# Where the causal mask of attention's score maxima is added: by TensorE's bfloat16 products, or by VectorE as it takes the maxima

## The chip, the core and the metric

The kernel runs on one core of a Trainium2 chip, in one launch. The metric is device time in microseconds from the launch's first to its last instruction; several runs are made and the median is given. The core's engines run side by side, each with its own queue in program order: TensorE (PE: matmuls, with its weight loads shown as PEld), VectorE (DVE), ScalarE (ACT), GpSimd (POOL) and SyncE (SP, which here issues the DMAs). Matmuls write to PSUM, eight banks of 512 float32 per partition; the other data lie in SBUF.

## What is computed

The reference passes a batch of 8 sequences of 512 tokens by 256 features through six residual layers: a feed-forward layer with four-bit quantisation, a retention layer, that feed-forward layer again, a soft mixture of experts, a causal attention with 16 heads of width 16, and the mixture of experts again. Every layer is preceded by a layer norm. The change touches the attention alone:

```python
scores = jnp.einsum('bhqd,bhkd->bhqk', q, k) / jnp.sqrt(jnp.float32(HEAD_DIM))
causal = jnp.tril(jnp.ones((S, S), dtype=bool))
scores = jnp.where(causal, scores, -jnp.inf)
attn = jax.nn.softmax(scores, axis=-1)
ctx = jnp.einsum('bhqk,bhkd->bhqd', attn, v)
```

with S = 512. Queries and keys come from projections with a low-rank part, which the kernel folds into one weight each.

## The kernel before

**Three lanes.** The program is one long sequence of instructions, written out by a planner while the kernel is built. Three lanes deliver steps: `front` (lane f: feed-forward, retention, feed-forward, and the routing of the first mixture), `back` (lane b: attention and the routing of the second mixture) and `experts` (lane e: the expert products). Lane f works on one sequence while lane b works on another. `Meter` (from line 82) keeps an estimate of when each engine is free and when each piece of data is ready; `drive` (line 1495) takes, among the lanes whose next step could begin, the one that the next letter of the string `ORDER` (line 67) names, and where no letter fits the one that has spent least (`chosen`, line 1464). Small work on VectorE that nobody needs at once is put off and slipped in where the planner sees room (`put_off`, `fill`). Because every instruction goes through the meter, the profile puts almost all of them on line 182; groups are told apart by the names of their tiles.

**PSUM.** It is divided into three pairs of banks (`pair`, line 327, kind "p") and two single banks (`one`, line 330, kind "o"), shared by all lanes. A step says which it needs ("pp" is two pairs) and starts when they are free.

**Attention** (line 1145) goes through a sequence's 16 heads in 4 head groups of 4 heads (index n). The four heads of a group lie in four blocks of 32 partitions, so that four products with a contraction of 32 rows run in TensorE at the same time. Each head group goes through this:

1. `largest(n, k)` for k = 0, 1, 2 (line 1218): the scores s_a, with queries as rows, for the query tiles named by `by_query` (line 1185): tiles 0 and 2 in stage 0, tile 3 in stage 1, tile 1 in stage 2. A query tile i has (i + 1) x 128 keys. `four` (line 1189) takes two pairs, writes each of the four heads into a bank of its own, and then adds the causal mask to the diagonal 128 x 128 block: one more product per head, the identity in bfloat16 (`identb`) against the mask in bfloat16 (`causalb`), accumulated into the same bank. In stage 0 it covers the diagonal blocks of both tiles, 256 columns. Then VectorE reduces: one instruction takes the negated maxima of two heads at once, so there are 4, 2 and 2 reductions in the three stages.
2. `lower(n)` (line 1238): when all three stages are done, VectorE transposes the 32 columns of maxima (`nmx`), four DMAs take them to HBM, and one brings them back as a row of the queries (`qv_a<-mx_a`). The queries hold a row that was left free for it, and the keys a row of ones, so that the next product subtracts the maxima.
3. `weights` and `exponentials` (lines 1258 and 1266) for three stages: the scores again, st_a, now with keys as rows; VectorE adds the float32 mask `causalT` in place (`masked`, line 1213), and ScalarE takes the exponential into pT_a.
4. `values` (line 1275): products with the values into c_a, whose extra column gives the sums; then a transpose on VectorE and the division.

The score stages of head group n + 1 are written between the stages of group n's weights, one each (line 1336), so the maxima are on their way while the previous group is worked on.

The constants are made at the start (lines 378 to 391): the identity, its bfloat16 copy, the two masks.

Of the kernel before, what the change touches and what calls it, by code (L numbers as in the profile page):

```python
# [21 lines left out]
BF = mybir.dt.bfloat16  # L22
I32 = mybir.dt.int32
AF = mybir.ActivationFunctionType
ALU = mybir.AluOpType
AX = mybir.AxisListType
PSUM = bass.MemoryType.PSUM

P = 128
D = 256  # L30
KD = D // P
S = 512
NT = S // P
# [31 lines left out]
SHARE = {"front": 1.0, "back": 0.9, "experts": 1.15}  # L65

ORDER = (
    "fffeeeeeffffbfbfbffbbbfbfffbbbeeeeeeebbfbfbebbfefefefbbebbebbbbfbfbfbfbbebffffbfffbfffffebebfbbfbfbf"
    "bfbebbbbbbbffffbffbfffbbfbbbbffffbfbbfbffbfffffbfbffbfbbfbbbbffffbffbbbfbfffbfbfbbfbfbfbfbfbbfbffbfe"
    "ebbbffbbbbffffffffffffffffffbfbffffbbbfebfeebbfbfffbfbfbbbffffbfbfbffbffbbbffbffbffbfbbffbbbbfffffff"  # L70
    "fffffffffffbbbbbffffffbfbfbbbfffbfffbbfbfbfbfffbbfbffbfbffbfebbbffbfbfbebffffbbbfbfffffffffffffffffb"
    "ffbffbbebebfbfbbbbbffffffbfbbffffffffbfbfebfbbffbffbfbbffbbbbffffffffffffffffffbfbbfbbffffbfbbfbbeff"
    "ffbebffebfbfbffbfffffbfbfbfbbfbfbfbfbfbbbbbbffffbfbffbfbfefffffffffeebebbbfffbbbbfbfbfbfbfffbfbbebbb"
    "fbfbfbbbbbbbbbb"
)

BEHIND = 60.0
# [217 lines left out]
def macaron(ctx: ExitStack, tc: tile.TileContext, a: dict, out: bass.AP):  # L295
    nc = Meter(tc.nc)
    B = out.shape[0]

    const = ctx.enter_context(tc.tile_pool(name="const", bufs=1))
# [27 lines left out]
    def pair(name):  # L327
        return take("p", name, [P, 2, 512])

    def one(name, keep=False):  # L330

        return take("o", name, [P, 512], keep)
# [45 lines left out]
    ident = const.tile([P, P], FP, tag="ident", name="ident")  # L378
    make_identity(tc.nc, ident)

    identb = const.tile([P, P], BF, tag="identb", name="identb")
    nc.vector.tensor_copy(identb, ident)

    causalb = const.tile([P, 2, P], BF, tag="causalb", name="causalb")
    causalT = const.tile([P, P], FP, tag="causalT", name="causalT")
    for t, pattern, cm in ((causalb, [[0, 2], [-1, P]], 1), (causalT, [[1, P]], -1)):
        nc.gpsimd.memset(t, 0.0)
        nc.gpsimd.affine_select(
            out=t, in_=t, pattern=pattern, compare_op=ALU.is_ge, fill=-1e30, base=0, channel_multiplier=cm
        )  # L390
    neghalf = const.tile([P, NS], FP, tag="neghalf", name="neghalf")
    nc.gpsimd.memset(neghalf, -0.5)
# [749 lines left out]
    NG = HPT // 2  # L1142
    VW = HD + 1

    def attention(lane, b, after):
        nm = f"a_{b}"
# [6 lines left out]
        qv, kv, nmx = {}, {}, {}  # L1153
# [15 lines left out]
        ps = pair(f"v_{nm}")  # L1169
# [11 lines left out]
        def rows_of(r):  # L1181
            return slice(32 * r, 32 * (r + 1))
# [3 lines left out]
        by_key = (((0, 0),), ((1, 0), (3, S - P)), ((2, 0),))  # L1186
        NK = len(by_key)

        def four(name, lhs, rhs, parts, mask, between=lambda: None):

            ps = [pair(f"{name}_{g}") for g in range(2)]
            bank = [ps[r // 2][:, r % 2, :] for r in range(NG)]
            for k, (ls, rs, to, _) in enumerate(parts):
                for r in range(NG):
                    nc.tensor.matmul(
                        bank[r][:, to], lhs[rows_of(r), ls], rhs[rows_of(r), rs], start=(k == 0), stop=mask is None and k == len(parts) - 1
                    )
            between()  # L1200
            if mask is None:
                return ps
            first, n = parts[0][3], len(parts)
            for r in range(NG):
                if n == 1:
                    at, m = bank[r][:, first : first + P], mask[:, 0, :]
                else:
                    step = (parts[1][3] - first) // P
                    at, m = bank[r].rearrange("p (c k) -> p c k", k=P)[:, first // P :: step, :], mask
                nc.tensor.matmul(at, identb, m, start=False, stop=True)  # L1210
            return ps

        def masked(ps, starts, by):
# [4 lines left out]
        def largest(n, k):  # L1218

            parts = []  # L1220
            if k == 0:
                nmx[n] = small.tile([P, BLK], FP, tag="nmx", name=f"nmx_{nm}_{n}")
                nc.gpsimd.memset(nmx[n], 0.0)
            for i, c in by_query[k]:
                w = (i + 1) * P
                parts.append((slice(i * P, w), slice(0, w), slice(c, c + w), c + w - P))
            ps = four(f"s_{nm}_{n}_{k}", qv[n], kv[n], parts, causalb)
            for g in range(2):
                for i, c in by_query[k]:
                    nc.vector.tensor_reduce(  # L1230
                        nmx[n][:, : NG * NT].rearrange("p (r i) -> p r i", i=NT)[:, 2 * g : 2 * g + 2, i],
                        ps[g][:, :, c : c + (i + 1) * P],
                        AX.X,
                        ALU.max,
                        negate=True,
                    )

        def lower(n):
# [19 lines left out]
        def weights(n, k, between=lambda: None):  # L1258

            parts, end = [], 0  # L1260
            for j, c in by_key[k]:
                end = c + S - j * P
                parts.append((slice(j * P, (j + 1) * P), slice(j * P, S), slice(c, end), c))
            return four(f"st_{nm}_{n}_{k}", kv[n], qv[n], parts, None, between), end

        def exponentials(n, k, ps, end):
            pT = []
# [7 lines left out]
        def values(n, k, pc, pT):  # L1275

            o, u = divmod(n, 2)
            for j, c in by_key[k]:
                for r in range(NG):
                    at = (j * HEADS + o * HPT + 2 * r + u) * VW  # L1280
                    nc.tensor.matmul(
                        pc[rows_of(r), j * P :],
                        va[:, at : at + 32],
                        pT[r // 2][:, r % 2, c : c + S - j * P],
                        start=(j == 0),
                        stop=(k == NK - 1),
                    )
# [28 lines left out]
        for k in range(NK):  # L1316
            yield "pp", (("qk", nm, 0),), ("s", nm, 0, k)
            largest(0, k)
        lower(0)

        yield "pp", (("qk", nm, 0),), ("s", nm, 1, 0)
        largest(1, 0)
        for n in range(N):
            for k in range(NK):
                if k == 0:
                    yield "ppo", (("q", nm, n), ("v", nm)), ("st", nm, n, k)
                    ps, end = weights(n, k)
                    pc = one(f"c_{nm}_{n}", keep=True)
                else:
                    yield "pp", (("q", nm, n), ("st", nm, n, k - 1)), ("st", nm, n, k)  # L1330
                    ps, end = weights(n, k, lambda: values(n, k - 1, pc, pT))
                pT = exponentials(n, k, ps, end)
                m, l = n + 1 + (k + 1) // NK, (k + 1) % NK
                if m < N and (n or l):
                    yield "pp", (("qk", nm, m // 2),), ("s", nm, m, l)
                    largest(m, l)
                    if l == NK - 1:
                        lower(m)
            yield "", (("st", nm, n, NK - 1), ("v", nm)), ("ctx", nm, n)
            values(n, NK - 1, pc, pT)  # L1340
            z = narrow(lane, f"z_{nm}_{n}", S)
            nc.vector.transpose(z, pc)
            divide_later(n, z)
            drop(f"c_{nm}_{n}")
            if n == 0:
                yield "p", (("yT", nm),), ("qk", nm, 1)
                qk(1)
                yield "pp", (("qk", nm, 1),), ("s", nm, 2, 0)
                largest(2, 0)
        for g in range(NT // 2):  # L1350
            yield "o", tuple(("cx", nm, o) for o in range(KD)), None
            ps = one(f"o_{nm}_{g}")
            for t in (2 * g, 2 * g + 1):
                for d in range(KD):
# [4 lines left out]
                        start=(d == 0),  # L1359
                        stop=(d == KD - 1),  # L1360
# [284 lines left out]
```

## Time and profile before

| What | Value |
|---|---|
| median of 3 runs | 2861.74 us (2860.11 to 2862.71) |
| profiled execution, first to last instruction | 2860.3 us |
| mean granted TensorE clock | 0.992 |
| score products s_a, 1024 instructions | busy 37.2 us (512 wide), 29.1 (384), 24.3 (256), 18.1 (128) |
| transposed score products st_a, 1024 | busy 37.6, 30.7, 26.3, 13.6 us for the same widths |
| loads of the bfloat16 identity, 384 | busy 24.6 us, mean 98 ns |
| TensorE idle until a reduction nmx_a let go | 4.5 us, 7 times |
| VectorE mask additions on st_a, 128x256, 256 | busy 101.3 us, mean 428 ns |
| VectorE idle until s_a was ready | 112.5 us, 57 times |
| ScalarE idle until st_a was masked | 150.0 us, 30 times |

In the page's groups a line has the source line, the engine, the operation, what it writes and reads (with tile names; the suffix tells the layer: _a attention, _m routing, _e experts, _f feed-forward, _r retention), the shapes and the number of instructions; after the first bar the busy time of the group and the mean length of one in ns; after the second the engine's idle time just before them and what ended it. A matmul's length holds its passage through a pipeline, so that lengths of neighbours overlap; what a group costs the queue is seen from the starts. For float32 operands each product is two instructions. The timeline gives the start, the length from the first start to the last end of a merged group, the engine and the operation. The bfloat16 products are one instruction each.

### The profile page before, as it was taken

Reading aid. Unit: us, or ns where it says so; the run is one execution under the profiler, and the core shown is the slowest. Engines: PE = TensorE matmul, PEld = TensorE weight load, DVE = VectorE, ACT = ScalarE, POOL = GpSimd, SP = SyncE. Lnnn points to the kernel's source line nnn. Section 1 sums busy time; section 2 is a strip of 40 time slices with the busy share of each in tenths; the row PEclk is TensorE's granted clock in tenths of the full one; section 3 lists DMA queues with packets and bytes.
Section 4 is the critical chain, followed back from the end, with each engine's and each line's share of the span. In section 5 each row is a group of like instructions: output and inputs, shape, how many; then the busy total and the mean of one; then the engine's idle time right before and its main releaser. Section 6 shows DMA issues by size and latency. Waiting matters only on the chain.

```text
span 2860.3 us, 34542 instructions
## 1 busy us (share of the span) xinstructions
PE 2753.0 (96%) x13166; PEld 1904.5 (67%) x13166; DVE 1675.2 (59%) x3989; ACT 1149.2 (40%) x1549; POOL 126.7 (4%) x260
## 2 busy tenths in 40 slices
PE   4889999999999999999999999999999999999999
PEld 2666677656776677666866667666677666665668
DVE  7787657555565674656746566466756655355440
ACT  2433434434434353433624435244443443434331
POOL 0000000000000000000000000000000000000000
PEclk9999999999999999999999999999999999999999
DMA  4000102110200320002200022000210020102020
GB/s 129 1 1 18 53 1 71 43 37 1 70 1 1 86 71 1 1 1 86 70 1 1 2 85 71 1 1 23 78 56 1 1 71 21 59 1 68 12 78 8
DMA packets 79015, 98.91 MB, mean 35 GB/s; under 512 B 17024, under 2 KB 63872, under 8 KB 78848
## 3 DMA queue, kind: packets, MB, share of 16 engines
q1 hardware_dynamic: 78848, 96.69, 11.5%
q8 instruction: 104, 1.70, 0.3%
q14 instruction: 63, 0.52, 0.1%
HBM read 58.40 MB, written 38.24 MB: 34 GB/s over the span
## 4 chain that ended last, share of the span: by engine, by line
PE 92%; DVE 4%; ACT 3%; issue 1%; DMA 0%; POOL 0%; ACTq 0%; POOLq 0%
PE p_e L182 15%; PE h_e L182 15%; PE gu_f L182 11%; PE lt_m L182 8%; PE mo_e L182 8%; PE sl_m L182 8%; PE dn_f L182 5%; PE s_a L182 4%; PE st_a L182 3%; PE c_a L182 3%; PE qk_a L182 2%; PE y_r L182 1%; PE a_r L182 1%; PE hTp_f L182 1%; PE k_r L182 1%; PE o_a L182 1%
## 5 line engine op out<-in xcount | busy, mean ns | idle before, releaser
L182 PE MATMUL h_e<-slT_m,w1g 128*128 128x256 f32 x2048 | 467.5, 383 | 9.6 <-ACT hid_e L182 4.6
L182 PE MATMUL p_e<-w,hid_e 128*128 128x256 f32 x2048 | 455.1, 381 | 1.5 <-DVE x L182 0.8
L182 PEld LDWEIGHTS h_e<-slT_m,w1g 128*128 128x128 f32 x2048 | 384.9, 191 | 85.1 <-issue 11.1
L182 PEld LDWEIGHTS p_e<-w,hid_e 128*128 128x128 f32 x2048 | 386.0, 190 | 62.1 <-issue 7.3
L182 ACT ACT_TABLE_LOAD x276 | 354.1, 1283 | 180.2 <-PE h_e L182 113.3
L182 PE MATMUL gu_f<-w_in,y_ffn 128*128 128x352 f32 x1024 | 327.0, 472 | 9.2 <-ACT y_ffn L182 8.0
L182 PEld LDWEIGHTS gu_f<-w_in,y_ffn 128*128 128x128 f32 x1024 | 196.7, 195 | 119.6 <-issue 12.9
L182 DVE TENSOR_REDUCE nmx_a<-s_a 128x2 f32<-128x256 f32 (+3 forms) x256 | 196.0, 819 | 113.0 <-PE s_a L182 112.5
L182 ACT ACTIVATE pT_a<-st_a 128x1024 f32<-128x1024 f32 (+1 forms) x192 | 158.8, 877 | 219.9 <-DVE st_a L182 150.0
L182 PE MATMUL lt_m<-yT_m,seT 128*128 128x512 f32 x512 | 231.0, 602 | 7.1 <-DVE lg_m L182 3.3
L182 PE MATMUL mo_e<-proc_e,lg_m 128*128 128x257 f32 x1024 | 234.3, 383 | 1.2 <-DVE x L182 1.2
L182 PE MATMUL sl_m<-ed_m,y_dis 128*128 128x512 f32 x512 | 227.5, 595 | 0.5 <-ACT y_ffn L182 0.5
L182 PEld LDWEIGHTS mo_e<-proc_e,lg_m 128*128 128x128 f32 x1024 | 190.8, 190 | 42.9 <-issue 4.8
L182 ACT ACTIVATE hid_e<-h_e 128x1024 f32<-128x1024 f32 x128 | 131.0, 1024 | 201.4 <-PE h_e L182 200.3
L182 ACT COPY proc_e<-p_e 128x512 f32<-128x512 f32 x64 | 37.5, 586 | 376.2 <-PE p_e L182 376.2
L182 PE MATMUL dn_f<-w_dn,hT_f 128*128 128x256 f32 x768 | 179.7, 386 | 1.1 <-ACT hT_f L182 1.0
L182 PEld LDWEIGHTS lt_m<-yT_m,seT 128*128 128x128 f32 x512 | 96.2, 192 | 121.3 <-issue 102.4
L182 PEld LDWEIGHTS sl_m<-ed_m,y_dis 128*128 128x128 f32 x512 | 96.1, 190 | 111.5 <-issue 102.6
L182 DVE TENSOR_TENSOR h_f<-h_f,gu_f 128x352 f32<-128x352 f32 x128 | 66.4, 519 | 167.1 <-ACT h_f L182 166.5
L182 PEld LDWEIGHTS dn_f<-w_dn,hT_f 128*128 128x128 f32 x768 | 144.5, 194 | 23.1 <-ACT hT_f L182 1.2
L182 DVE TENSOR_SCALAR_CACHE_REDUCE lg_m<-lt_m 128x512 f32<-128x512 f32 x128 | 85.3, 683 | 124.9 <-PE lt_m L182 124.9
L182 DVE TENSOR_TENSOR st_a<-st_a,causalT 128x256 f32<-128x256 f32 x256 | 101.3, 428 | 70.1 <-PE st_a L182 67.0
(190 smaller groups left out, 3132.0 us busy)
## 6 DMA issues: line engine op xcount, KB each, us to landing
d_ed_m<-ed_m SPq DMA_DIRECT2D x256, 128.0 KB
ed_m<-d_ed_m SPq DMA_DIRECT2D x64, 512.0 KB
rb_m<-row_rb_m SPq DMA_DIRECT2D x32, 256.0 KB
x<-in_L_attn_x SPq DMA_DIRECT2D x8, 512.0 KB
tm_m<-row_nm_m SPq DMA_DIRECT2D x16, 256.0 KB
out<-x SPq DMA_DIRECT2D x8, 512.0 KB
row_rb_m<-z_rb_m SPq DMA_DIRECT2D x128, 0.5 KB
mx_a<-z_mx_a SPq DMA_DIRECT2D x128, 2.0 KB
```

Source lines behind the costliest of these rows:

```text
L182: call(*args, **kwargs)
```

## The change

The mask products go. `four` no longer has a mask, and the bfloat16 identity is not made. `causalb` becomes one tile of 128 x 512 in bfloat16: zero in the first 384 columns, the causal pattern in the last 128. In `largest`, the reduction of two heads is replaced by one fused VectorE instruction per head and query tile (`tensor_tensor_reduce`): it adds the last w columns of `causalb` to the head's w columns of scores, multiplies by -1, writes that back in place, and takes the minimum, starting from 3e38, into the head's column of `nmx`. That is the same negated maximum in the same place. So for one head group there are 8, 4 and 4 fused instructions in the three stages. `ORDER` is another string (621 letters instead of 615). The meter's prices are not changed.

```diff
--- before.py
+++ after.py
@@ -65,13 +65,13 @@
 SHARE = {"front": 1.0, "back": 0.9, "experts": 1.15}
 
 ORDER = (
-    "fffeeeeeffffbfbfbffbbbfbfffbbbeeeeeeebbfbfbebbfefefefbbebbebbbbfbfbfbfbbebffffbfffbfffffebebfbbfbfbf"
-    "bfbebbbbbbbffffbffbfffbbfbbbbffffbfbbfbffbfffffbfbffbfbbfbbbbffffbffbbbfbfffbfbfbbfbfbfbfbfbbfbffbfe"
-    "ebbbffbbbbffffffffffffffffffbfbffffbbbfebfeebbfbfffbfbfbbbffffbfbfbffbffbbbffbffbffbfbbffbbbbfffffff"
-    "fffffffffffbbbbbffffffbfbfbbbfffbfffbbfbfbfbfffbbfbffbfbffbfebbbffbfbfbebffffbbbfbfffffffffffffffffb"
-    "ffbffbbebebfbfbbbbbffffffbfbbffffffffbfbfebfbbffbffbfbbffbbbbffffffffffffffffffbfbbfbbffffbfbbfbbeff"
-    "ffbebffebfbfbffbfffffbfbfbfbbfbfbfbfbfbbbbbbffffbfbffbfbfefffffffffeebebbbfffbbbbfbfbfbfbfffbfbbebbb"
-    "fbfbfbbbbbbbbbb"
+    "fffbeeeeffffbfbfbffbbbfbfffbbbbbebbeeebfbefbebbfbfefefbbffebbfbbbfbfbbbbbbbefffffbfffbfffffebebfbbfb"
+    "fbfbfbebbfbbbfffffbffbfbefbfbfffbfbfbbbfbfffbfffffbfbffbfbbfbbbbffbffffbbbebfffbffbbbfbfbfbfbbbfbffb"
+    "feebbbbbbbbbbfbbffffffffffffffbffbfffbbbbbbeebbfbfffffbbbbbffffbfbffffbbfbbbffbfbffbbfbbfbbffffbffef"
+    "ffbbfbbbbfbbbbfbbbbfffffffffbbbffffffbbbfbbbbfffbbffffbfbffbfebbfbfbfffbebffffbbbbbffffbffffffffffff"
+    "bffbffbbfbebebbfbbbbfffbffbfbbffffffffffbbbfeefffbbbfbbfbbfbbbbbbbbbbffbfffbffffbffefbbfbbfffffbfefe"
+    "bfbfbfebfbfebbbbffbffffffbbffffbfbbbfbffbfbfbbbbffffbbfbbffbfeffffbffefbfffffffbfffbffbbfffbbbbbbbbb"
+    "bbfbfbbbbbbfbbbbbbbbb"
 )
 
 BEHIND = 60.0
@@ -378,15 +378,13 @@
     ident = const.tile([P, P], FP, tag="ident", name="ident")
     make_identity(tc.nc, ident)
 
-    identb = const.tile([P, P], BF, tag="identb", name="identb")
-    nc.vector.tensor_copy(identb, ident)
-
-    causalb = const.tile([P, 2, P], BF, tag="causalb", name="causalb")
+    causalb = const.tile([P, S], BF, tag="causalb", name="causalb")
     causalT = const.tile([P, P], FP, tag="causalT", name="causalT")
-    for t, pattern, cm in ((causalb, [[0, 2], [-1, P]], 1), (causalT, [[1, P]], -1)):
-        nc.gpsimd.memset(t, 0.0)
+    nc.gpsimd.memset(causalb, 0.0)
+    nc.gpsimd.memset(causalT, 0.0)
+    for t, step, cm in ((causalb[:, S - P :], -1, 1), (causalT, 1, -1)):
         nc.gpsimd.affine_select(
-            out=t, in_=t, pattern=pattern, compare_op=ALU.is_ge, fill=-1e30, base=0, channel_multiplier=cm
+            out=t, in_=t, pattern=[[step, P]], compare_op=ALU.is_ge, fill=-1e30, base=0, channel_multiplier=cm
         )
     neghalf = const.tile([P, NS], FP, tag="neghalf", name="neghalf")
     nc.gpsimd.memset(neghalf, -0.5)
@@ -1186,28 +1184,16 @@
         by_key = (((0, 0),), ((1, 0), (3, S - P)), ((2, 0),))
         NK = len(by_key)
 
-        def four(name, lhs, rhs, parts, mask, between=lambda: None):
-
-
+        def four(name, lhs, rhs, parts, between=lambda: None):
 
             ps = [pair(f"{name}_{g}") for g in range(2)]
             bank = [ps[r // 2][:, r % 2, :] for r in range(NG)]
-            for k, (ls, rs, to, _) in enumerate(parts):
+            for k, (ls, rs, to) in enumerate(parts):
                 for r in range(NG):
                     nc.tensor.matmul(
-                        bank[r][:, to], lhs[rows_of(r), ls], rhs[rows_of(r), rs], start=(k == 0), stop=mask is None and k == len(parts) - 1
+                        bank[r][:, to], lhs[rows_of(r), ls], rhs[rows_of(r), rs], start=(k == 0), stop=k == len(parts) - 1
                     )
             between()
-            if mask is None:
-                return ps
-            first, n = parts[0][3], len(parts)
-            for r in range(NG):
-                if n == 1:
-                    at, m = bank[r][:, first : first + P], mask[:, 0, :]
-                else:
-                    step = (parts[1][3] - first) // P
-                    at, m = bank[r].rearrange("p (c k) -> p c k", k=P)[:, first // P :: step, :], mask
-                nc.tensor.matmul(at, identb, m, start=False, stop=True)
             return ps
 
         def masked(ps, starts, by):
@@ -1223,16 +1209,15 @@
                 nc.gpsimd.memset(nmx[n], 0.0)
             for i, c in by_query[k]:
                 w = (i + 1) * P
-                parts.append((slice(i * P, w), slice(0, w), slice(c, c + w), c + w - P))
-            ps = four(f"s_{nm}_{n}_{k}", qv[n], kv[n], parts, causalb)
-            for g in range(2):
+                parts.append((slice(i * P, w), slice(0, w), slice(c, c + w)))
+            ps = four(f"s_{nm}_{n}_{k}", qv[n], kv[n], parts)
+            for r in range(NG):
                 for i, c in by_query[k]:
-                    nc.vector.tensor_reduce(
-                        nmx[n][:, : NG * NT].rearrange("p (r i) -> p r i", i=NT)[:, 2 * g : 2 * g + 2, i],
-                        ps[g][:, :, c : c + (i + 1) * P],
-                        AX.X,
-                        ALU.max,
-                        negate=True,
+                    w = (i + 1) * P
+                    own = ps[r // 2][:, r % 2, c : c + w]
+                    at = r * NT + i
+                    nc.vector.tensor_tensor_reduce(
+                        own, own, causalb[:, S - w :], -1.0, 3e38, ALU.add, ALU.min, nmx[n][:, at : at + 1]
                     )
 
         def lower(n):
@@ -1260,8 +1245,8 @@
             parts, end = [], 0
             for j, c in by_key[k]:
                 end = c + S - j * P
-                parts.append((slice(j * P, (j + 1) * P), slice(j * P, S), slice(c, end), c))
-            return four(f"st_{nm}_{n}_{k}", kv[n], qv[n], parts, None, between), end
+                parts.append((slice(j * P, (j + 1) * P), slice(j * P, S), slice(c, end)))
+            return four(f"st_{nm}_{n}_{k}", kv[n], qv[n], parts, between), end
 
         def exponentials(n, k, ps, end):
             pT = []
```

## The prediction

> **What bounds the kernel now.** I read the page first: which engine is full, and whether its clock is. Then the chain that ended last.
>
> ```profile
> span 2860.3 us, 34542 instructions
> PE 2753.0 (96%) x13166; PEld 1904.5 (67%) x13166; DVE 1675.2 (59%) x3989; ACT 1149.2 (40%) x1549; POOL 126.7 (4%) x260
> PE 92%; DVE 4%; ACT 3%; issue 1%; DMA 0%; POOL 0%; ACTq 0%; POOLq 0%
> ```
>
> TensorE is the bound. Its 107 us of idle time lie mostly in the weight preparation: adding up the idle time ahead of TensorE's groups in the timeline from 440 us to the end gives 36.6 us in 2420, so it is 98.5% busy where attention runs (first score at 514 us, last reduction at 2673). A microsecond of matmul removed there is worth a microsecond, as long as nothing new makes TensorE wait. The part of the chain that ended last which covers attention is a sequence of matmul groups too, with single VectorE pieces between.
>
> Next the groups by shape, for the operations that the change takes out, and for those nearest to what it puts in.
>
> ```profile
> L182 PE MATMUL s_a<-causalb,identb 128*128 128x128 bf16 x256 | 25.4, 222 | 0.0
> L182 PE MATMUL s_a<-causalb,identb 128*128 128x256 bf16 x128 | 20.4, 284 | 0.0
> ...
> L182 DVE TENSOR_REDUCE nmx_a<-s_a 128x2 f32<-128x1024 f32 x64 | 75.4, 1220 | 51.4 <-PE s_a L182 51.4
> L182 DVE TENSOR_REDUCE nmx_a<-s_a 128x2 f32<-128x768 f32 x64 | 60.8, 949 | 0.0
> L182 DVE TENSOR_REDUCE nmx_a<-s_a 128x2 f32<-128x512 f32 x64 | 41.2, 686 | 27.8 <-PE s_a L182 27.6
> L182 DVE TENSOR_REDUCE nmx_a<-s_a 128x2 f32<-128x256 f32 x64 | 26.9, 420 | 33.8 <-PE s_a L182 33.6
> L182 DVE TENSOR_TENSOR aT_r<-a_r,dec 128x512 f32<-128x512 f32 x8 | 5.5, 692 | 49.3 <-PE a_r L182 49.3
> L182 DVE TENSOR_TENSOR aT_r<-a_r,dec 128x384 f32<-128x384 f32 x8 | 4.4, 549 | 0.0
> L182 DVE TENSOR_TENSOR aT_r<-a_r,dec 128x256 f32<-128x256 f32 x8 | 3.4, 422 | 3.3 <-PE a_r L182 3.1
> L182 DVE TENSOR_TENSOR aT_r<-a_r,dec 128x128 f32<-128x128 f32 x8 | 2.2, 280 | 0.0
> L182 DVE DVE_READ_ACCUMULATOR lg_m<-lt_m 128x1 f32 x128 | 10.6, 83 | 0.0
> ```
>
> The mask products are 45.8 us of busy time, the reductions 204.3 us. A busy matmul is pipelined, so 45.8 is not what their removal frees. That is read from starts, in the timeline of TensorE around one group (start, length, engine):
>
> ```profile
> 545.03 1.14 PE L182 MATMUL s_a<-kv_a,qv_a 32*128 32x512 f32 x8
> 546.10 0.40 PE L182 MATMUL s_a<-causalb,identb 128*128 128x128 bf16 x4
> 546.34 1.95 PE L182 MATMUL p_e<-w,hid_e 128*128 128x256 f32 x8
> ...
> 623.72 1.14 PE L182 MATMUL st_a<-qv_a,kv_a 32*128 32x512 f32 x8
> 624.79 1.57 PE L182 MATMUL mo_e<-proc_e,lg_m 128*128 128x257 f32 x6
> ```
>
> Scores start at 545.03, the mask 1.07 us later, the next work 0.24 after that. The transposed scores below have the same shape and no mask, and the next full-array matmul starts 1.07 us after them too.
>
> **Term 1, mask products out.** There are 96 groups (8 sequences, 4 head groups, 3 stages). Going through all of them in that timeline, an undisturbed mask holds TensorE for 0.45 us in the 32 groups of stage 0 (four products 256 wide) and 0.235 us in the 64 others (128 wide). 32 x 0.45 + 64 x 0.235 = 29.4 us. The 384 loads of the bf16 identity lie inside these intervals. In 17 groups (2 and 15) TensorE then waits for something anyway, 11.5 us in all, so the mask is covered there: 2 x 0.45 + 15 x 0.235 = 4.4 us that are not won. Net 25 us. The upper end is 34.3 us, the sum of all intervals with their slow cases (0.498 and 0.283 us on average).
>
> The Trainium skill, TensorEngine Tiling (Array Packing), Key Properties, says that a change of tiling mode drains TensorE; by it one could credit a drain saved in each group besides. The two starts of 1.07 us say no: the drain stays with whatever full-array matmul follows. Only where 32-row or 32-column work follows does a switch go (0.54 instead of 0.45 us before c_a), under 1 us in all, which I leave out.
>
> **Term 2, VectorE's work.** Per head group, 8 reductions over two heads each become 16 fused operations over one: in stage 0 four of 128 and four of 384 columns, in stage 1 four of 512, in stage 2 four of 256. With 32 head groups (8 sequences of 4) that is 128 of each width, 512 instead of 256, each with an accumulator to be read out. The trace has no such operation. Three prices:
> - Lowest: like the reduction with accumulator of the dispatch logits (512 wide, from PSUM, followed by an accumulator read). In VectorE's timeline the read comes 0.61 us after the start and the next reduction follows at once. The aT_r rows give (692 - 280) / 384 = 1.073 ns per element, so 0.549 us of stream and 0.06 fixed. Stage 0: 2048 x 1.073 ns + 8 x 0.06 = 2.68 us against 2.49 measured for its four reductions; stage 1: 2.44 against 2.35; stage 2: 1.34 against 1.28. Together 0.34 us more, x 32 = 11 us.
> - Middle: like the mask addition on st_a, in place in PSUM with a second operand: two of 256 in 0.76 us at 536.60, so the second starts 0.76 - 0.428 = 0.33 us after the first, 0.06 fixed; and the accumulator read at its full 83 ns. Stages 3.34, 2.77, 1.67 us: 0.85 + 0.42 + 0.39 = 1.66 more, x 32 = 53 us.
> - Highest: row sums without overlap: 128 x (280 + 422 + 549 + 692) ns + 512 x 83 ns = 291 us against 204.3: 87 us.
>
> I take 53 us, by the row nearest in operands and place. VectorE goes from 59% to about 61%; in the stretch 500 to 650 us it is busy 83.7 of 150 us, and in none of the attention stretches that I looked at over two thirds. It does not become the bound.
>
> What can reach TensorE is the release of PSUM. A score group holds two of the three pairs until its last reduction. Without the mask VectorE can begin 0.45 or 0.24 us earlier, and then takes 0.85, 0.42, 0.39 us longer: the hold grows by 0.40, 0.18 and 0.15 us. Queued behind on VectorE are the mask additions on st_a (ScalarE's exponential waits for them), the logits' reductions and the gate products; and the transpose of the maxima, whose five DMAs on SP's queue bring the row that the next st_a needs, which is fetched a head group ahead. TensorE waits after 17 of 96 groups now: 17 x 0.24 (mean of the three) = 4 us. Its other waits for VectorE from 440 us on sum to 27 us; VectorE's free share falls from 41 to 39%, so about 5% of them, 1.5 us. Both ends: nothing, if the row's price is the lowest; and 17 x 0.6 + 27 us = 37 us if the price is the highest (87 - 29 us of hold over 96 groups = 0.6) and its other waits double.
>
> The Trainium skill, VectorE: DVE Perf Modes, Rules for kernel authors, advises to cut the number of VectorE operations, since each pays a pipeline flush; this change doubles it. With that page's (N + 151) / 0.96 ns for a tensor_tensor the fused operations would be an estimated 251 us before the reads, close to the highest price; the sum would then be some 7 us worse than mine. The 0.33 us from start to start against 428 ns of length shows that part of that flush is overlapped here.
>
> **Small parts, at nothing.** The bf16 identity's cast (304 ns, VectorE) goes; causalb doubles to 512 columns (a 311 ns memset on GpSimd becomes an estimated 0.6). Both lie before 3 us, and TensorE's first matmul starts at 14.0, after the first weights' DMA. Uncovered it would be 0.3 us. The maxima land in the same columns, so the transpose and its DMAs stay as they are.
>
> **The order of the lanes.** It moves whole steps among the three lanes; no instruction count changes. What a row can bound is the idle time that an order leaves: at best part of the 36.6 us, at worst as much again. I take 0: nothing in the profile says which way.
>
> **Sum.** -25 + 4 + 1.5 = -19.5 us on the profiled execution's 2860.3, so 2840.8; the median of the runs is 1.4 us above that span, so **2842 us**. Its own range is 2828 to 2855.
>
> **Rivals.**
> - *More than the sum* (chance 0.15): the mask's whole 34 us and a third of the idle time through the order: 2862 - 34 - 12, about 2815. For it: 79 of the 96 masks are followed by work that waits for nothing. Against: the 17 waits would have to go as well.
> - *No change* (0.10): the saved matmul time turns up as waits for PSUM pairs at once, as in the 17 groups: 2856 to 2867. For it: three pairs only, and score groups take two. Against: the same 79 groups.
> - *VectorE's longer hold decides* (0.27, slower): one place, the last fused operation of a score group before its pair comes free. At the highest price the hold grows by 0.6 us per group; if TensorE meets it in three of four groups, 72 x 0.6 = 43 us against 25 won: 2880. It decides from about 42 groups on (42 x 0.6 = 25), or, at an operation half as fast per element as the rows (32 x 5120 elements x 1.073 ns = 176 us more, 1.8 us per group), from 14 groups on. For it: ScalarE already idles 150 us for the additions on st_a. Against: VectorE itself idles 112.5 us waiting for s_a, which it now gets earlier.
>
> **How the numbers follow.** The forecast has 0.48. Its 0.48 and the first rival's 0.15 are faster; a measurement here tells 0.2%, 5.7 us, from no change, so faster 0.63, same 0.10, slower 0.27. The range reaches down to the first rival's 2815 and up to 2884 in the third; some 0.15 lies outside, mostly above.
>
> **What would show it.** No causalb product on TensorE, and 12 matmuls fewer per head group there; starts of s_a to the next full-array matmul of 1.07 us; 512 fused VectorE operations with a sum of 250 to 295 us with their reads; VectorE at 60 to 62%; TensorE's busy time near 2707 and its idle time within 10 us of 107. I am wrong if the fused row of 512 is well over 0.8 us, if TensorE's waits for nmx_a or for st_a grow past 20 us, or if its idle time moves by more than that in stretches without attention, which would be the order.

## The result, and the profile after

The changed kernel takes 2869.47 us (median of 9 runs, 2868.32 to 2869.97) where the kernel before takes 2861.74 (9 runs, 2860.10 to 2862.74). The ratio is 1.0027, with a 95% interval from 1.0018 to 1.0037: slower by 7.7 us, where 2842 and a gain of 19.5 us were forecast. That is above the forecast's own range (2828 to 2855) and above that of *no change* (to 2867); it lies inside the whole range of 2815 to 2884, in the part that belonged to the third rival.

The page's first lines and its chain, of the changed kernel (busy time, share of the span, instructions):

```profile
span 2867.7 us, 34547 instructions
PE 2735.4 (95%) x12782; PEld 1883.9 (66%) x12782; DVE 1748.1 (61%) x4756; ACT 1130.7 (39%) x1535; POOL 126.3 (4%) x260
PE 86%; DVE 8%; ACT 4%; issue 2%; SPq 0%; DMA 0%; POOL 0%; ACTq 0%; DVEq 0%; POOLq 0%
```

The 384 products are gone, and yet TensorE's busy time falls by 17.6 us (by 31.8 in e1 below, which puts nothing in their place), its idle time grows from 107 to 132 us, and VectorE's part of the chain that ended last doubles from 4% to 8%.

The groups by shape that took the place of the reductions:

```profile
L182 DVE CUSTOM_DVE_ANT_0 s_a<-s_a,causalb 128x512 f32<-128x512 f32 x128 | 87.9, 706 | 47.2 <-PE s_a L182 38.4 <-ACT yT_m L182 3.7 <-ACT pT_a L182 1.3
L182 DVE CUSTOM_DVE_ANT_0 s_a<-s_a,causalb 128x384 f32<-128x384 f32 x128 | 72.5, 566 | 4.4
L182 DVE CUSTOM_DVE_ANT_0 s_a<-s_a,causalb 128x256 f32<-128x256 f32 x128 | 53.7, 439 | 35.0 <-PE s_a L182 32.7
L182 DVE CUSTOM_DVE_ANT_0 s_a<-s_a,causalb 128x128 f32<-128x128 f32 x128 | 39.3, 307 | 48.8 <-PE s_a L182 46.6
L182 DVE DVE_READ_ACCUMULATOR2_ANT nmx_a<- 128x1 f32 x512 | 72.4, 141 | 0.0
```

Each is 14 to 27 ns longer than the aT_r row of its width, and the read that follows takes 141 ns, not 83. How they stand in VectorE's queue is seen from the starts, in its timeline for one stage 1 of the changed kernel:

```profile
522.69 0.70 DVE L182 CUSTOM_DVE_ANT_0 s_a<-s_a,causalb 128x512 f32<-128x512 f32 x1 [3.67 <-ACT yT_m L182]
523.31 0.14 DVE L182 DVE_READ_ACCUMULATOR2_ANT nmx_a<- 128x1 f32 x1
523.49 0.70 DVE L182 CUSTOM_DVE_ANT_0 s_a<-s_a,causalb 128x512 f32<-128x512 f32 x1
524.10 0.14 DVE L182 DVE_READ_ACCUMULATOR2_ANT nmx_a<- 128x1 f32 x1
524.10 0.73 DVE L182 CUSTOM_DVE_ANT_0 s_a<-s_a,causalb 128x512 f32<-128x512 f32 x1
524.75 0.14 DVE L182 DVE_READ_ACCUMULATOR2_ANT nmx_a<- 128x1 f32 x1
524.93 0.70 DVE L182 CUSTOM_DVE_ANT_0 s_a<-s_a,causalb 128x512 f32<-128x512 f32 x1
```

The second operation starts only when the first one's read is over (523.31 + 0.14, then 523.49), the third, which is the first of the second pair of banks, together with the read before it, and the fourth waits again: 0.80, 0.61 and 0.83 us from start to start. Counted from its first start to that of the next instruction, where one follows at once, a stage takes 3.88, 2.85 and 1.96 us (stages 0, 1 and 2, medians) where the reductions took 2.40, 2.27 and 1.32. That is 2.70 us more per head group and 86 us in all.

TensorE's waits for VectorE, in the list of its waits (who waits, for whom, total, times, longest), again of the changed kernel:

```profile
PE h_e L182 <- DVE nmx_a L182: 7.2, 7, 1.3
PE st_a L182 <- DVE nmx_a L182: 7.0, 6, 1.7
...
PE gu_f L182 <- DVE nmx_a L182: 2.4, 2, 1.3
```

That is 16.6 us in 15 waits for a pair that the fused operations still hold, against 4.5 us in 7 waits before.

### The profile page after: what moved, and what is told of

Same layout as the page of the kernel before. It is cut to its first block, busy times and chain, and to the rows that moved or that the text cites. A ratio compares the mean times of both kernels' runs of the same rounds, so it can differ in the third digit from the quotient of the medians.

```text
span 2867.7 us, 34547 instructions
## 1 busy us (share of the span) xinstructions
PE 2735.4 (95%) x12782; PEld 1883.9 (66%) x12782; DVE 1748.1 (61%) x4756; ACT 1130.7 (39%) x1535; POOL 126.3 (4%) x260
## 4 chain that ended last, share of the span: by engine, by line
PE 86%; DVE 8%; ACT 4%; issue 2%; SPq 0%; DMA 0%; POOL 0%; ACTq 0%; DVEq 0%; POOLq 0%
PE p_e L182 15%; PE h_e L182 14%; PE gu_f L182 10%; PE lt_m L182 8%; PE mo_e L182 8%; PE sl_m L182 7%; PE dn_f L182 5%; PE st_a L182 3%; PE c_a L182 2%; PE s_a L182 2%; PE qk_a L182 2%; DVE s_a L182 2%; PE hTp_f L182 1%; PE a_r L182 1%; PE y_r L182 1%
## 5 line engine op out<-in xcount | busy, mean ns | idle before, releaser
L182 PE MATMUL h_e<-slT_m,w1g 128*128 128x256 f32 x2048 | 467.0, 382 | 10.2 <-DVE nmx_a L182 7.2
L182 DVE CUSTOM_DVE_ANT_0 s_a<-s_a,causalb 128x128 f32<-128x128 f32 (+3 forms) x512 | 250.7, 505 | 135.4 <-PE s_a L182 117.8
L182 ACT COPY proc_e<-p_e 128x512 f32<-128x512 f32 x64 | 37.5, 586 | 332.4 <-PE p_e L182 332.4
L182 PEld LDWEIGHTS dn_f<-w_dn,hT_f 128*128 128x128 f32 x768 | 144.1, 193 | 25.3 <-issue 3.1
```

The source lines that it names most:

```text
L182: call(*args, **kwargs)
```

## The experiments

Two things changed together, the work and the order of the lanes. To separate them, the experiments keep the order: a helper tells the planner of the instruction that stood in the old program, and puts another one, or none, in its place. So in each experiment every other instruction of every engine comes in the order of the kernel named.

```python
    def instead(self, name, op, call, *args, **kwargs):
        if name == "PE" and self.kept:
            self.flush()
            self.kept = []
        if name != "PE" and self.kept is not None:
            self.kept.append((name, op, call, args, kwargs))
        else:
            self.emit(name, op, call, args, kwargs)
```

**e1, the products out, nothing in their place.**

```diff
-                nc.tensor.matmul(at, identb, m, start=False, stop=True)
+                nc.instead("PE", "matmul", lambda *x, **y: None, at, identb, m, start=False, stop=True)
...
-        "head_mask": np.where(own, HD**-0.5, 0.0),
+        "head_mask": np.where(own, HD**-0.5 / 4, 0.0),
```

> The kernel before, its instructions in the order of before, without the 384 mask products; the reductions stay. The causal mask of the maxima is left out, and the scores are scaled down by four more so that the sums stay above zero. Theory A (the products hold TensorE for 29 us, and the loss lies in the fused work on VectorE): 2826 to 2840, with TensorE's idle time near 100 us. Theory C (the products were mostly covered, so their removal frees little): above 2852.

Measured: 2841.59 us (5 runs, 2840.48 to 2842.10), ratio 0.9933 (0.9919 to 0.9946), so 18.8 us less than the 2860.41 of the runs beside it. By the starts in TensorE's timeline the work in its queue falls by 31.5 us; its idle time grows by 11 us (102 to 113, both added up from that timeline). So theory C falls, and theory A's price for the masks was somewhat high (its range ended at 2840): a good third of the freed time comes back at once, as waits that the masks had covered.

**e2, the fused operations alone.** The masks stay on TensorE; `zero` is a tile of zeros made at the start.

```diff
-                    nc.vector.tensor_reduce(
+                    def both(*x, g=g, i=i, c=c, nmx=nmx[n], ps=ps, **y):
+                        w = (i + 1) * P
+                        for r in (2 * g, 2 * g + 1):
+                            own = ps[g][:, r % 2, c : c + w]
+                            at = r * NT + i
+                            tc.nc.vector.tensor_tensor_reduce(
+                                own, own, zero[:, :1].to_broadcast([P, w]), -1.0, 3e38, ALU.add, ALU.min, nmx[:, at : at + 1]
+                            )
+
+                    nc.instead(
+                        "DVE", "tensor_reduce", both,
```

> The kernel before with its mask products and in its order; only the 256 reductions become 512 fused operations (they add zeros, as the mask is there already). Theory A (their longer time on VectorE reaches TensorE): 2890 to 2905, TensorE idle 30 to 45 us longer. Theory B (the fused work costs little, the new order of the lanes costs what was won): 2862 to 2870.

Measured: 2884.61 us (4 runs), ratio 1.0084 (1.0070 to 1.0098): 24.2 us more. Less than theory A said, far more than theory B. By the pages TensorE's idle time grows by 14 us (107 to 121), not by 30 to 45; the other 10 us are busy time.

**e3, the change without its order.** The edits of e1 (without the smaller scale) and e2 together, with the causal tile instead of the zeros.

> Masks out of TensorE and into the fused operations, as in the change, but every instruction in the order of before. Theory A: 2862 to 2876, as the changed kernel. Theory B: 2836 to 2848, as I forecast for the change without its order.

Measured: 2874.32 us (5 runs), ratio 1.0046 (1.0034 to 1.0059). Theory A holds.

**e4, the order without the change.** The changed kernel's plan, with the old products and reductions put in place of the fused operations.

> The old work (mask products and reductions of two heads) laid out in the order of the changed kernel. Theory A: 2856 to 2868, the order matters little. Theory B: 2880 to 2895, the order alone costs 20 us or more.

Measured: 2874.61 us (5 runs), ratio 1.0046 (1.0034 to 1.0059). Both expectations missed: the new order costs the old work 14.2 us. The four corners, in us:

| | mask by products | mask by fused operations |
|---|---|---|
| order of before | 2860.4 (kernel before) | 2874.3 (e3) |
| new order | 2874.6 (e4) | 2869.5 (changed kernel) |

The new order is worth 4.9 us to the changed work (6.2 when each is compared with the kernel before of its own session, 2860.4 for e3 and 2861.7 for the changed kernel) and costs 14.2 to the old, so the order is not where the gain went. In the order of before, with the mask off TensorE, going from the reductions (e1) to the fused operations (e3) costs 32.7 us.

**e5 and e6, what in the fused operations costs it.** They add idle work on VectorE to e1, of the length by which the fused operations exceed the reductions: in e5 after a stage's last reduction, where it holds no PSUM, in e6 split before the last reduction of each pair. BEFORE stands for False in e5 and for True in e6; the lines that e5 and e6 share with e1 are left out here.

```diff
+                    def reduced(*x, g=g, i=i, c=c, k=k, **y):
+                        last = i == by_query[k][-1][0]
+                        w = (1330, 605, 560)[k] // (2 if BEFORE else 1)
+                        if BEFORE and last:
+                            tc.nc.vector.tensor_reduce(waste, w_in[:, 0, :w], AX.X, ALU.max)
+                        tc.nc.vector.tensor_reduce(*x, **y)
+                        if not BEFORE and last and g:
+                            tc.nc.vector.tensor_reduce(waste, w_in[:, 0, :w], AX.X, ALU.max)
```

> As e1 (no mask products, reductions of two heads, order of before, mask left out, scores scaled down by four more), with idle work added on VectorE: after the last reduction of each stage one more reduction over a weight in SBUF, about 1.49, 0.71 and 0.66 us long in stages 0, 1 and 2, 92 us in all, which is what the fused operations took beyond the reductions. It holds no PSUM. Theory H (what costs is that the PSUM pairs are released later): 2842 to 2852, near e1's 2841.6. Theory L (what costs is that VectorE is later for everybody, wherever its work lies): 2866 to 2878, near e3's 2874.

> As e5, but the same idle work lies half before the last reduction of the first pair and half before that of the second, so the pairs are released later by about as much as with the fused operations. Theory H and theory L both: 2866 to 2878, near e3's 2874. The difference from e5 is the price of the later release alone: 20 to 30 us by H, under 6 us by L.

Measured: e5 2857.61 us (11 runs, of which ten from 2857.2 to 2860.8 and one, the profiled one, 2852.9), e6 2868.03 (11 runs, 2865.7 to 2869.6); against before 0.9989 (0.9980 to 0.9998) and 1.0024 (1.0015 to 1.0033). Neither theory holds alone. Each against the kernel before of its own session (2860.4 for e1 and e3, 2861.2 for e5 and e6), e1 takes 18.8 us less, e5 3.6 less, e6 6.8 more and e3 13.9 more. So VectorE's load without any PSUM held costs 15.2 us; holding the pairs longer costs 10.4 more; 7.1 us remain up to e3, where the fused operations also write back and read an accumulator each. Counted like the 86 us above, the added work is 85 us in e5 and 94 in e6 (the 92 in the expectation came from a coarser count), so a part of the 10.4 can be the 9 us that e6 does more.

How the later release looks, in TensorE's timeline of e1 and then of e3, at the same place of the same order:

```profile
584.98 1.14 PE L191 MATMUL st_a<-qv_a,kv_a 32*128 32x512 f32 x8
587.50 3.72 PE L191 MATMUL h_e<-slT_m,w1g 128*128 128x256 f32 x16 [1.38 <-ACT hid_e L191]
```

```profile
580.37 3.72 PE L191 MATMUL h_e<-slT_m,w1g 128*128 128x256 f32 x16 [0.45 <-DVE qv_a L191]
584.92 1.13 PE L191 MATMUL st_a<-qv_a,kv_a 32*128 32x512 f32 x4 [0.83 <-DVE nmx_a L1257]
586.88 2.08 PE L191 MATMUL st_a<-qv_a,kv_a 32*128 32x512 f32 x4 [0.83 <-DVE nmx_a L1257]
588.88 6.01 PE L191 MATMUL h_e<-slT_m,w1g 128*128 128x256 f32 x16
```

In e1 eight products of st_a run as one group. In e3 they come in two fours, each waiting 0.83 us for a pair that the fused operations of the next head group's scores still hold. Then something else appears: the second four take 2.08 us instead of 1.13, and sixteen products h_e 6.01 us instead of 3.72. The clock has been halved, as e3's table of stretches shows (start and end, length, busy time and instructions of PE, PEld, DVE, ACT and POOL, granted clock, DMA share, GB/s):

```profile
583.30:586.70 3.40, 1.92 (x8) 0.66 (x6) 3.23 (x15) 2.31 (x2) 0.00 (x0) 1.00 0.19 70
586.70:593.50 6.80, 6.62 (x15) 4.22 (x16) 3.10 (x6) 4.50 (x4) 0.00 (x0) 0.50 0.01 4
593.50:596.90 3.40, 3.40 (x13) 2.05 (x12) 0.00 (x0) 1.95 (x2) 0.00 (x0) 0.99 0.00 0
```

The clock records of the traces, added up from 440 us to the last stretch, give this time at half clock: before 13.7 us, e1 6.8, e2 17.1, e4 13.7, e5 10.2, e6 34.1, e3 37.5, e7 10.2, the changed kernel 27.3. A microsecond at half clock loses half a microsecond of matmul work. From e1 to e3 that is (37.5 - 6.8) / 2 = 15 us of the 31.5 us between the two profiled executions; by the pages 9 more are idle time of TensorE, and the other 7 are busy time that the clock does not account for. From e5 to e6 it is (34.1 - 10.2) / 2 = 12 us of the 16.2 between the profiled executions, while TensorE's idle time does not grow (128 and 126 us). But e5's profile is of its fastest run, with a mean clock of 0.992 where the other ten have 0.989 to 0.991; so the clock's part of the 10.4 us between the medians is smaller, and some of e5's own 15.2 is clock.

Each of the nine stretches at half clock in e3 after 440 us begins right behind 3.4 us in which TensorE idled for 1.3 to 2.5 us, like the first line above. That the waits cause it remains an inference; no run varied the clock alone. Such idle time is not enough by itself: from 576.0 to 579.4 us e3 idles 1.7 us and the clock stays whole. And e2, which still has the mask products between, waits as long for nmx_a as e3 (12.3 us in 16 waits against 11.6 in 15) and spends less than half as long at half clock. What tips it, no run shows.

**e7, a cheaper mask on TensorE.** What e1 frees can be had in part without VectorE. The maximum needs no exact mask: softmax cancels a small shift. So a product over 32 rows will do, in which the row of a block of four keys holds powers of two: for the query's own key it adds -1/16, for the next -512, for later ones more, and next to nothing for earlier ones. Each head's product lies in its own 32 rows, like its scores.

```diff
-                nc.tensor.matmul(at, identb, m, start=False, stop=True)
+                mine = rows_of(r)
+                nc.instead(
+                    "PE", "matmul",
+                    lambda *x, at=at, m=m, mine=mine, **y: tc.nc.tensor.matmul(at, identb[mine, :], m[mine], start=False, stop=True),
+                    at, identb, m, start=False, stop=True
+                )
...
+    block, at = np.arange(P) // 4, np.arange(P) % 4
+    row = (np.arange(P) % 32)[:, None]
+    q = np.where(block == row, 2.0 ** (-13.0 * at), 0.0)
+    k = np.where(block == row, -(2.0 ** (13.0 * at - 4)), np.where(block > row, -(2.0**80), 0.0))
```

> Mask products stay on TensorE, in the order of before, but each contracts 32 rows of a small bfloat16 factorisation of the mask (powers of two, so that a key one ahead of the query is lowered by 512 and the query's own by 1/16) in its head's 32-row block, so the four run at the same time and in the tiling of the scores. VectorE's work is that of before. If the 0.235 and 0.45 us per group of before are the four full-array products one after another, a group now takes 0.06 to 0.12 us: 20 to 25 us of TensorE freed, of which by e1 (33.5 freed, 18.8 won) a bit over half shows: 2846 to 2853. If 32-row bfloat16 products do not overlap, no gain: 2858 to 2863.

Measured: 2847.59 us (5 runs, 2846.17 to 2849.73), ratio 0.9955 (0.9942 to 0.9967): 13.6 us less than before, and 21.9 less than the changed kernel. TensorE's timeline of e7 around the group that the prediction showed:

```profile
544.41 1.14 PE L191 MATMUL s_a<-kv_a,qv_a 32*128 32x512 f32 x8
545.38 0.23 PE L1228 MATMUL s_a<-causalb,identb 32*128 32x128 bf16 x4
545.54 2.64 PE L191 MATMUL p_e<-w,hid_e 128*128 128x256 f32 x11
```

From the scores' start to the next work it is 1.13 us, where it was 1.31 with the full mask and 1.07 without one. The mask now stays in the scores' 32-row tiling, and the step to the full array comes after it. Over the run, scores and mask together hold TensorE's queue for 25.3 us less (104.1 instead of 129.4, from starts). The 33.5 us that the expectation takes from e1 are 31.5 by the count above; a bit over half of what is freed shows here too (13.6 of 25.3).

## Why the prediction was wrong

**What bounds the kernel** was read rightly: TensorE is the bound, and work taken from its queue shortens the run (e1, e7).

**Term 1, mask products out, net 25 us.** Queue time of 29.4 to 34.3 us was forecast, 31.5 was freed. The cover was mis-sized: I counted the 17 groups after which TensorE already waited and charged 4.4 us for them. In e1 11 us came back as idle time, and 18.8 us were won. Waits that the masks had hidden came out in other groups too: those for VectorE's logits grew from 5.0 to 8.9 us, those for ScalarE's hid_e from 8.1 to 10.1.

**Term 2, VectorE's work, 53 us of it and 5.5 us in the time: this is the step that failed.** The work was under-priced: 86 us by starts, which is my highest price (87), not the middle one. A fused operation does not overlap with the read of the one before it as the logits' reduction does (0.61 us there; 0.80, 0.61 and 0.83 here), and the read is longer. The larger error was what a microsecond on VectorE costs. I let it act through the 17 known waits and through 5% of the others (whose 27 us already held the 4.5 for nmx_a; without them it is 22). In e5 VectorE's load alone costs 15.2 us for 85 of work, e6 puts 10.4 on the later release, and e3 is 32.7 above e1: 38% of the 86 us added to an engine that is 59% busy reaches the end. And the sum had no term for TensorE's clock, which it took as it was: that is 15 of the 31.5 us between the profiles of e1 and e3. An average share says little about a queue in program order: what stands behind the added work is late whenever it is wanted soon after, and TensorE has only three pairs to get round it. The upper end that the working named for this term, 37 us, would have covered it.

**The drain.** That taking out the mask saves no change of tiling was right: e1 frees the mask's interval and no more. The rule of the Trainium skill, VectorE: DVE Perf Modes, Rules for kernel authors, to cut the number of VectorE operations, spoke against this change, and the runs side with it more than I did: 1024 instructions in place of 256 took 86 us more.

**The order of the lanes, 0.** Between e3 and the changed kernel it is worth 4.9 us, well inside the bounds given.

In sum: 2860.4 - 18.8 + 32.7 (both in the order of before) - 4.9 for the order = 2869.4. This sum closes because its terms are differences between the same runs; it is no check of them.

**The rivals.** The third named the direction and one half of the mechanism, the pairs that come free later; its point of decision, 42 groups that TensorE meets, was not what decided: TensorE waits for a pair 15 times. In e6 the later release gives 10.4 us; the other shares are VectorE's load itself and TensorE's clock, which no rival named. *More than the sum* is excluded; *no change* only just (7.7 us against its 5.7, and the interval reaches down to 0.18%).

**The signs named beforehand.** The fused rows with their reads sum to 326 us (253.4 + 72.4) instead of 250 to 295, VectorE is at 61% as said, TensorE's busy time is 2735 us instead of near 2707, and its idle time grew by 25 us, not by less than 10. The waits for nmx_a (16.6 us) and the fused row of 512 (706 ns) stay under the limits named.

## What to carry to other kernels

Work moved off a full engine to one with 40% to spare is not free: price it by a run that adds the same length of idle work at the same place of the order, not by the free share. Compare new work in the old order before the order is searched again, or the two effects hide one another (here the same letters cost the old work 14 us and saved the changed work 5). And a mask that only guards a maximum can be coarse: in low rank, in the tiling of the products that it follows, it took less time than either exact form here.

## What the runs showed of the hardware

- The clock fell without a long pause. The Trainium skill, TensorE: Matmul & The Clock Gate, Why this matters for your kernels, says that gaps of more than some 3 us between bursts of matmuls bring the half clock back. In e3 no wait of TensorE after 440 us was longer than 2.6 us, and it spent 37.5 us at half clock; in the stretch shown, two waits of 0.83 us around four 32-row products came just before it. The measurement differs from the rule: waits shorter than its figure came before half clock here.
- Half clock came in pieces of 3.4 or 6.8 us, and the slow rows lie in them: in e3 from 586.7 to 593.5 us, with st_a at 586.88 and h_e at 588.88 above; in the changed kernel from 910.6 to 914.0, with st_a at 910.2 (1.75 us for sixteen instead of 1.15) and c_a at 911.9 (1.94 for eight instead of 1.06).
- The fused operation's accumulator read took 141 ns against 83 ns for the built-in reduction's. Within a pair of banks the next fused operation always started after the end of that read; where it was the first on the second pair, it started together with the read in 93 of 96 stages of the changed kernel. Whether the engine or a wait of the program makes the difference, no run shows.
